# Two cross-attention layers in float32: the last batch's mean from an extra product column, and a bias sum moved from VectorE to ScalarE and adding transfers

## The chip, the cores and the metric

The kernel runs on one core of a Trainium2 chip. The metric is device time in microseconds: the time of one execution of the whole program, input loads and output stores included. Its median over three runs is compared. Beside these times there is one profiled execution, with a record of every instruction of every engine; its span, from first to last record, is shorter than its device time.

A core has TensorE (PE, with PEld for the loading of its stationary operand), VectorE (DVE), ScalarE (ACT) and GpSimd (POOL). SyncE (SP) here only issues transfers; ScalarE and GpSimd issue some too. Each engine takes its own instructions in order and waits at semaphores for the others.

## The reference

There are 8 batches of 100 queries with 1024 features, and a context of 1444 rows of 512 features for each batch. Everything is float32.

```
layer 0:  Q = x Wq + bq;  K = c Wk + bk;  V = c Wv + bv
          x = x + (softmax over keys of (Q K^T / 32)) V Wo + bo
layer 1:  q = x Wq + bq;  k = c Wk + bk;  v = c Wv + bv
          w = softmax over QUERIES of (q k^T / 32)
          x = w v + x
          out = (x - mean) * (var + 1e-6)^-1/2 * gamma + beta    (over the 1024 features)
```

Mean and variance of a query need all 1024 features of its row. The kernel uses that Q K^T = x (Wq Wk^T) c^T plus bias terms and that the value path is (softmax c)(Wv Wo) plus bias terms, so it first multiplies the weights with each other. The term bv Wo, a vector of 1024, belongs to the output bias of layer 0. It is the sum over 1024 rows of Wo, each times one element of bv.

## The kernel before

**Stages.** In order of time: Wq Wk^T of layer 0 (`weight_products`, "qk0", to 52 us), Wv Wo of layer 0 ("vo0", 52 to 100 us), the projected queries of layer 0 ("g0", 100 to 137 us), Wq Wk^T of layer 1 ("qk1", to 184 us), the scores, softmax and weighted rows of layer 0 for the 8 batches (to about 350 us), the last of the value projection of layer 0 (`project0`, "o0", to 381 us), the projected queries of layer 1, and then the batches of layer 1. There the batches form the sets 0 to 3, 4 to 6 and 7. For each batch `alternated` interleaves, on TensorE, the weighted rows of this batch (A) with the scores of the batch two ahead (s). After the first two sets `project1` multiplies their A with Wv; for the last batch `project_last` does it.

**The order of the work.** TensorE's order is the order in which the Python code issues products (`manual_schedule`). For the other engines the framework orders instructions by its own estimate, except for those that are kept in program order: VectorE's between `vector.in_order = True` and `False` (all go through the helper on line 96), and some of ScalarE's. A tile comes from a pool with a number of buffers; the first writer of a reused buffer waits for the last reader of what was in it. The pool `stream` has 10 buffers, for weights, context rows and context columns; in layer 1 two of them hold gamma, beta and the value bias.

**Products with fewer multiplications.** The large products are split in 2x2 blocks and made with seven block products instead of eight. That needs sums of blocks (S1.., T1..) on VectorE before a product, and evictions that put or add one PSUM result into several output blocks. For vo0 (lines 464 to 530) the products come in the order X, Z, Y, X again, and then W and Q, which are split once more and interleaved with a last product into X. The second X product reads S2, four tiles that overwrite S1, which the Y product before it reads, and T2. `put` copies a result by ScalarE, `add` adds it by VectorE. In `project0` (lines 1082 to 1090) one of the seven products, W, is split again in seven steps. The steps x, z, y, x, w, y, x share three PSUM banks; `run(W)` issues the steps that are left.

**The bias sum.** `transferred_sum` makes bv Wo as eight scaled tiles of 128x1024. For "qk1" ScalarE scales all eight (`scaled_sum`) and transfers that add into SBUF, issued by GpSimd (`transfer_added`, line 567), sum them as a tree. For "qk0" and "vo0" ScalarE and such transfers do four; VectorE does the other four in `second_half`, one multiplication and three multiply-adds into one tile, which a last transfer adds to the first. In vo0 `second_half` is called between T2 and the addition of Z. The transposing sum that uses the result (`block_sums`, "bvo") runs in the g0 stage.

**The last batches.** `untransposed` turns x back to queries by features with eight transposes on TensorE and adds the value bias (line 1192, z, two halves of 512). `normalise` follows: statistics by VectorE (line 1198), aggregated (1203), the variance plus epsilon (1205), the power -1/2 on GpSimd (1206), then (z - mean) gamma on VectorE (1207). For all batches but the last, ScalarE multiplies by the power (1209), GpSimd adds beta (1210) and the output leaves (1212). Batches 4, 5 and 6 are finished while A of batch 7 is made. For batch 7 `project_last` makes A Wv in three parts of 512, 384 and 128 columns (1232), adds each to z (1233) and takes its statistics; after the power VectorE makes the two output halves (1215), whose transfers SP and ScalarE issue (1216).

Of the kernel before, what the change touches and what calls it, by code (L numbers as in the profile page):

```python
# [25 lines left out]
F32 = mybir.dt.float32  # L26
AF = mybir.ActivationFunctionType
ALU = mybir.AluOpType
# [27 lines left out]
def two_layer_cross_attention(ctx: ExitStack, tc: tile.TileContext, a: dict, out: bass.AP):  # L56
# [17 lines left out]
    def unit(name):  # L74
        return stream.tile([P, E + L], F32, tag="unit", name=name)
# [4 lines left out]
    def row(name):  # L80
        return work.tile([P, E], F32, tag="row", name=name, bufs=3)
# [58 lines left out]
    def run(*parts):  # L140

        parts = list(parts)
        while parts:
            parts = [g for g in parts if next(g, parts) is not parts]
# [202 lines left out]
    def weight_products(name, left, right, l_width, r_width, scaled, between=None):  # L347
# [87 lines left out]
        def put(r, c, banks):  # L435
            for j in range(2):
                nc.scalar.copy(block(r, c, j), banks[j].rearrange("p (n w) -> p n w", n=per))  # L437

        def add(r, c, banks):
            for j in range(2):  # L440
                to = block(r, c, j)
                vector.tensor_tensor(to, to, banks[j].rearrange("p (n w) -> p n w", n=per), ALU.add)
# [21 lines left out]
        if name == "vo0":  # L464
            accumulate(1)
        put(0, 0, X)
        vector.in_order = name == "vo0"
        combine(T1, B12, B11, ALU.subtract)
        if name == "qk0":
# [26 lines left out]
        if name != "qk0":  # L496
            T2, T4 = B11, B21
            combine(T2, B22, T1, ALU.subtract)
            if name == "vo0":
                accs[scaled[0][0]][1]()  # L500
            add(0, 0, Z)
        combine(S1, S1, A11, ALU.subtract)
        S2 = S1
        if name != "vo0":
            combine(A21, A11, A21, ALU.subtract)
        if name != "qk0":
# [36 lines left out]
    def transferred_sum(name, srcs, of):  # L543

        n = EC if of == "qk1" else EC // 2
        tiles = [row(f"{name}_{n}") for n in range(2)] + [weight_rows(f"{name}_2")[:, :E]]
        tiles += [t[:, :E] for t in prob]  # L550
        if n == EC:
            tiles += [weight_rows(f"{name}_{n}")[:, :E] for n in range(6, 8)]
        scaled_sum(tiles[:n], srcs[:n])

        def second_half():
            t = tiles[n]
            for i, (src, by) in enumerate(srcs[n:]):
                if i == 0:
                    vector.tensor_scalar(t, src, by, None, ALU.mult)
                else:  # L560
                    vector.scalar_tensor_tensor(t, src, by, t, ALU.mult, ALU.add)
            transfer_added(tiles[0], t)

        return tiles[0], second_half
# [4 lines left out]
    def scaled_sum(tiles, srcs):  # L569

        for t, (src, by) in zip(tiles, srcs):
            tc.keep_in_program_order(nc.scalar.activation(t, src, AF.Copy, scale=by))
        k = 1
        while k < len(tiles):
            for i in range(0, len(tiles) - k, 2 * k):
                transfer_added(tiles[i], tiles[i + k])
            k *= 2
# [435 lines left out]
    def project0(AS, A0):  # L1013
# [65 lines left out]
        add(1, 1, 1, Y)  # L1079
        product(X_, S_[1], T2, False)  # L1080

        next(W)
        add(1, 0, 1, X_)
        run(W)
        add(1, 0, 1, Y)
# [62 lines left out]
    def project1_sums(w):  # L1148
        t = weights.tile([P, LC, E], F32, tag="w", name="wv1_s")
        A = [[w[:, 2 * k + i, h * 512 : h * 512 + 512] for i in range(2)] for h in range(2) for k in range(2)]  # L1150
        S = [[t[:, n, i * 512 : i * 512 + 512] for i in range(2)] for n in range(4)]
        left_sums(A, S, engine=nc.gpsimd)
        return A, S
# [38 lines left out]
            nc.vector.scalar_tensor_tensor(z[:, half], bv1[j][:T], s["r"], ps[:T, :], ALU.mult, ALU.add)  # L1192
        yield

    def statistics(s, j, part, parts):
        if j == 0:
            s["stats"] = small.tile([T, parts, 6], F32, tag=f"stats{parts}", name=f"stats_{s['b']}")
        nc.vector.bn_stats(s["stats"][:, j, :], s["z"][:, part])

    def normalise(s):  # L1200
        b, z = s["b"], s["z"]
        mv = small.tile([T, 2], F32, tag="mv", name=f"mv_{b}")
        nc.vector.bn_aggr(mv, s["stats"].rearrange("p a n -> p (a n)"))
        rstd = small.tile([T, 1], F32, tag="rstd", name=f"rstd_{b}")
        nc.vector.tensor_scalar(rstd, mv[:, 1:2], EPS, None, ALU.add)  # L1205
        nc.gpsimd.tensor_tensor(rstd, rstd, mhalf[:T], ALU.pow)  # L1206
        nc.vector.scalar_tensor_tensor(z, z, mv[:, 0:1], gamma[:T], ALU.subtract, ALU.mult)
        if b < B - 1:
            nc.scalar.activation(z, z, AF.Copy, scale=rstd)  # L1209
            nc.gpsimd.tensor_tensor(z, z, beta[:T], ALU.add)  # L1210

            (nc.gpsimd if b < SETS[1][0] else nc.sync).dma_start(out=out[b], in_=z)
            return
        for half, queue in ((slice(0, E // 2), nc.sync), (slice(E // 2, E), nc.scalar)):
            nc.vector.scalar_tensor_tensor(z[:, half], z[:, half], rstd, beta[:T, half], ALU.mult, ALU.add)
            queue.dma_start(out=out[b][:, half], in_=z[:, half])

    def finish(s):

        yield from untransposed(s)  # L1220
        for j in range(2):
            statistics(s, j, slice(j * 512, (j + 1) * 512), 2)
        normalise(s)

    def project_last(s, A):

        parts = (slice(0, 512), slice(512, 896), slice(896, E))
        for j, part in enumerate(parts):
            n = part.stop - part.start
            ps = bank(f"ol_{j}")  # L1230
            for k in range(LC):
                nc.tensor.matmul(ps[:T, :n], A[:, k, :T], wv1[:, k, part], start=(k == 0), stop=(k == LC - 1))
            nc.vector.tensor_tensor(s["z"][:, part], s["z"][:, part], ps[:T, :n], ALU.add)
            statistics(s, j, part, len(parts))
        normalise(s)


    batches = [{"b": b} for b in range(B)]
# [94 lines left out]
    for bs in SETS:  # L1333
        t = wide(f"A1T_{bs[0]}").rearrange("p c t -> p (c t)")[:, : LC * len(bs) * T]
        t = t.rearrange("p (c t) -> p c t", c=LC)
        for i, b in enumerate(bs):
            for n, _ in enumerate(alternated(b, 1, softmax1, t[:, :, i * T : (i + 1) * T])):
                if b % 2 and n == (8 if b == B - 1 else 27):
                    weight_totals(batches[b - 1 : b + 1])
                if (b, n) in finished:  # L1340
                    finishing.append(finish(batches[finished[b, n]]))
                finishing = [f for f in finishing if next(f, finishing) is not finishing]
            if b == 1:
                AS = project1_sums(wv1)
        if b < B - 1:

            between, room = {3: (batches[5], (0, 3, 3, 3, 3)), 6: (batches[7], (1, 0, 0, 1, 2))}[b]
            project1(bs, *AS, t, between["softmax"], room)
    run(untransposed(batches[B - 1]))
    project_last(batches[B - 1], t)  # L1350


# [22 lines left out]
```

## Time and profile before

| | us |
|---|---|
| median of three runs (633.78 to 634.80) | 634.42 |
| the profiled execution | 634.84 |
| its span | 632.9 |
| TensorE busy | 621.5 (98%) |
| VectorE busy | 487.1 (77%) |
| ScalarE busy | 163.9 (26%) |
| GpSimd busy | 102.2 (16%) |

The granted clock of TensorE is 0.997 of full speed. Transfers move 138.27 MB, a mean of 218 GB/s.

How to read it: a line of a timeline has the start and the duration in us, engine, line of the code, operation, output <- inputs, shapes and the count of merged instructions. In square brackets stands how long the engine stood idle before, and for whom. A float32 product is two matmul records for each pair of tiles, so "x16" are eight products. Line 96 is the helper of all VectorE instructions that can be kept in order, so these are told apart by their tiles. Durations of neighbours on one engine overlap by some 0.1 us. A line of the waits has engine, waiting tile and line <- engine, tile and line waited for, then us in total, times, and the longest.

### The profile page before, as it was taken

What the parts mean: (1) busy time and instruction counts of PE and PEld (TensorE: products, weight loads), DVE (VectorE), ACT (ScalarE), POOL (GpSimd) and SP (SyncE); (2) the same over time, 40 slices, a digit from 0 to 9 for tenths busy, and PEclk for the clock granted to TensorE, in tenths of its full rate; (3) what the DMA queues carried; (4) which work ended last, traced back from release to release, by engine and by line L of the source; (5) the groups of instructions that cost most, each with busy time, mean ns of one, the idle gap of its engine ahead of it and who ended that gap; (6) DMA issues with size and microseconds to landing.
All of it is one profiled execution on the core that took longest, in us unless ns stands there. A gap on an engine that the chain in (4) does not pass through costs nothing.

```text
span 632.9 us, 10570 instructions
## 1 busy us (share of the span) xinstructions
PE 621.5 (98%) x4142; PEld 534.2 (84%) x4142; DVE 487.1 (77%) x995; ACT 163.9 (26%) x380; POOL 102.2 (16%) x133
## 2 busy tenths in 40 slices
PE   9999999999999999999999999999999999999994
PEld 8886467688985999999989666756999999999992
DVE  2987979996885797666758687968777659898886
ACT  1322012324304234423230001113433240325301
POOL 2110101112230000000000001008111220544054
PEclk9999999999999999999999999999999999999998
DMA  8969848335999788988942308255888990599002
GB/s 272 293 136 348 274 140 272 68 81 111 203 315 382 283 311 299 327 307 306 312 155 88 101 0 325 96 194 192 295 305 307 316 324 2 201 330 332 27 22 84
DMA packets 52521, 138.27 MB, mean 218 GB/s; under 512 B 4403, under 2 KB 8755, under 8 KB 52471
## 3 DMA queue, kind: packets, MB, share of 16 engines
q1 hardware_dynamic: 46792, 120.85, 55.1%
q0 software_dynamic: 5280, 16.26, 11.7%
q8 instruction: 33, 0.54, 0.3%
q10 hardware_dynamic: 398, 0.47, 0.2%
q14 instruction: 18, 0.14, 0.1%
HBM read 123.36 MB, written 3.28 MB: 200 GB/s over the span
## 4 chain that ended last, share of the span: by engine, by line
PE 90%; DMA 3%; DVE 3%; issue 1%; POOL 1%; ACT 0%; POOLq 0%; DVEq 0%; SPq 0%
PE s L923 25%; PE A L894 25%; PE qk_x L163 6%; PE o_x L163 5%; PE g_x L163 4%; DMA vo<-in_L_xattn_Wo 3%; PE o_y L163 3%; PE g_y L163 3%; PE vo_x L163 2%; PE qk_y L163 2%; PE qk_z L163 2%; DVE vo L96 1%; PE o_z L163 1%; PE o_w L163 1%; PE qk_w L163 1%
## 5 line engine op out<-in xcount | busy, mean ns | idle before, releaser
L894 PE MATMUL A<-w,c 120*128 120x100 f32 (+1 forms) x1536 | 249.6, 265 | 0.0
L894 PEld LDWEIGHTS A<-w,c 120*128 120x128 f32 (+1 forms) x1536 | 218.0, 190 | 2.8
L96 DVE STREAM_TRANSPOSE w<-prob 32x384 f32<-32x384 f32 (+1 forms) x256 | 143.7, 561 | 27.6 <-ACT prob L962 9.7
L923 PE MATMUL s<-cT,g1T 128*100 128x131 f32 (+2 forms) x592 | 122.8, 296 | 0.0
L923 PE MATMUL s<-cT,g0T 128*100 128x131 f32 (+2 forms) x592 | 122.7, 296 | 0.0
L923 PEld LDWEIGHTS s<-cT,g1T 128*100 128x100 f32 x592 | 78.4, 167 | 8.6 <-issue 0.3
L923 PEld LDWEIGHTS s<-cT,g0T 128*100 128x100 f32 x592 | 78.2, 167 | 8.4 <-PE c L593 0.4
L935 ACT ACTIVATE prob<-s,c 100x393 f32<-100x393 f32 (+2 forms) x64 | 34.5, 560 | 112.7 <-PE s L923 99.5
L1111 ACT ACTIVATE w<-w,negmax 120x100 f32<-120x100 f32 (+1 forms) x96 | 34.8, 364 | 82.7 <-DVE negmax L96 82.7
L955 DVE TENSOR_REDUCE maxima<-prob 100x1 f32<-100x394 f32 (+3 forms) x32 | 16.5, 528 | 23.4 <-ACT prob L935 23.1
L1321 POOL DMA_DIRECT2D wv<-in_L_xattn_Wv x1 | 0.8, 772 | 191.2 <-PE o_x L163 191.2
L163 PE MATMUL qk_x<-qk 128*128 128x256 f32 x128 | 29.7, 380 | 0.0
L1130 POOL TENSOR_TENSOR part<-w 120x500 f32<-120x500 f32 x8 | 10.9, 1368 | 112.9 <-DVE rstd L1205 28.6
L163 PEld LDWEIGHTS qk_x<-qk 128*128 128x128 f32 x128 | 23.3, 190 | 3.0 <-ACT qk L437 0.2
L669 ACT ACTIVATE g1T<-g_x,k 128x400 f32<-128x400 f32 x4 | 2.4, 594 | 69.2 <-PE g_x L163 69.0
L1111 ACT ACTIVATION_READ_ACCUMULATOR w<-w,negmax 120x1 f32 (+1 forms) x96 | 17.9, 187 | 0.0
L1210 POOL TENSOR_TENSOR z<-z,vectors 100x1024 f32<-100x1024 f32 x7 | 16.5, 2356 | 8.2 <-ACT z L1209 8.2
L96 DVE TENSOR_TENSOR xT<-xT,o_x 128x400 f32<-128x400 f32 (+1 forms) x32 | 15.8, 539 | 2.2 <-PE o_x L163 2.0
L1188 PE MATMUL z<-ident,xT 128*100 128x128 f32 x64 | 16.3, 273 | 0.0
L1209 ACT ACTIVATE z<-z,rstd 100x1024 f32<-100x1024 f32 x7 | 8.0, 1149 | 31.9 <-POOL rstd L1206 31.9
L1192 DVE SCALAR_TENSOR_TENSOR z<-vectors,r,z 100x512 f32<-100x512 f32 x16 | 11.8, 740 | 4.8 <-PE z L1188 4.8
L163 PE MATMUL vo_x<-vo 128*128 128x512 f32 x32 | 15.3, 595 | 0.0
(415 smaller groups left out, 987.8 us busy)
## 6 DMA issues: line engine op xcount, KB each, us to landing
cT<-in_ctxT SPq DMA_DIRECT2D x64, 722.0 KB, 6.3
c<-in_ctx SPq DMA_DIRECT2D x48, 768.0 KB, 8.3
c<-in_ctx SPq DMA_DIRECT2D x16, 512.0 KB, 5.9
vo<-in_L_xattn_Wo SPq DMA_DIRECT2D x8, 512.0 KB, 10.1
qk<-in_L_xattn_WqT SPq DMA_DIRECT2D x8, 512.0 KB
qk<-in_L_xattn_WqT SPq DMA_DIRECT2D x15, 256.0 KB, 5.8
c<-in_ctx SPq DMA_DIRECT2D x16, 224.0 KB, 5.9
xT<-in_xT SPq DMA_DIRECT2D x2, 1600.0 KB
```

The lines of the kernel that those rows point to most:

```text
L96: ins = getattr(nc.vector, op)(*args, **kw)
L163: nc.tensor.matmul(banks[n // per][:, n % per * width : (n % per + 1) * width], lhs[i][:, n * P : (n + 1) * P], rhs[i], start=(fresh and i ...
L894: nc.tensor.matmul(ps[:, k * T : (k + 1) * T], c[m // CQ][:r, m % CQ, k * P : (k + 1) * P], w[:r, m, :], start=(m == 0 and k == 0), stop=( ...
L923: nc.tensor.matmul(banks[n // per][:T, cuts[n] - o : cuts[n + 1] - o], q[:, k, t0 : t0 + T], cT[k][:, cuts[n] : cuts[n + 1]], start=(k == ...
L935: nc.scalar.activation(p[:, part], ps[:T, : part.stop - part.start], AF.Identity, bias=key_bias[layer][:T, b : b + 1], scale=SCALE,)
L955: nc.vector.tensor_reduce(maxima[:, n : n + 1], p[:, part], AX.X, ALU.max)
L1111: nc.scalar.activation(w[:r, m0 + m, :], w[:r, m0 + m, :], AF.Exp, bias=negmax[:r, m : m + 1], accum_out=total[:r, m : m + 1])
L1130: add(part, w[:MR, 0:5, :], w[:MR, 5:10, :], ALU.add)
L1188: nc.tensor.transpose(ps[:T, e * P : (e + 1) * P], xT[:, 4 * j + e, b * T : (b + 1) * T], ident)
L1192: nc.vector.scalar_tensor_tensor(z[:, half], bv1[j][:T], s["r"], ps[:T, :], ALU.mult, ALU.add)
L1209: nc.scalar.activation(z, z, AF.Copy, scale=rstd)
L1210: nc.gpsimd.tensor_tensor(z, z, beta[:T], ALU.add)
```

## The change

1. vo0: the second four tiles of the bias sum are scaled by ScalarE, right after it has put the first product, and summed by three more adding transfers; VectorE's four instructions are gone. The addition of Z moves behind the four instructions that make S2. Two of the tiles take buffers of `weight_rows`.
2. project0: four steps of W rather than one are issued ahead of the addition of X_, so VectorE's two additions of X_ come after W's first four.
3. Layer 1: after the work of batch 6, `last_columns` copies the first 383 columns of Wv into a new tile and puts the row sums of Wv, by ScalarE's accumulator, in the 384th column. In the built order these five instructions stand among the evictions of batch 7's scores. The two tiles come from `stream`.
4. `project_last`: parts of 383 (with the extra column, 384), 512 and 129 columns. The mean comes from the extra column and two ScalarE sums of z. Each part is centred as it comes, squared and summed by ScalarE; the parts are multiplied by gamma meanwhile. The statistics instructions, the aggregate and the full-width (z - mean) gamma are gone. A last ScalarE instruction forms the variance, GpSimd takes the power.
5. `normalise` for batch 6: the multiplication by the power and the addition of beta are one VectorE instruction, instead of ScalarE's and GpSimd's. In the built order it stands on VectorE between the two instructions that make the mean of batch 7.

```diff
@@ weight_products @@
         put(0, 0, X)
+        if name == "vo0":
+            accs[scaled[0][0]][1]()
         vector.in_order = name == "vo0"
...
             combine(T2, B22, T1, ALU.subtract)
-            if name == "vo0":
-                accs[scaled[0][0]][1]()
-            add(0, 0, Z)
+            if name != "vo0":
+                add(0, 0, Z)
         combine(S1, S1, A11, ALU.subtract)
         S2 = S1
+        if name == "vo0":
+            add(0, 0, Z)
@@ transferred_sum @@
-        if n == EC:
+        if of != "qk0":
             tiles += [weight_rows(f"{name}_{n}")[:, :E] for n in range(6, 8)]
         scaled_sum(tiles[:n], srcs[:n])
         def second_half():
             t = tiles[n]
-            for i, (src, by) in enumerate(srcs[n:]):
...
+            if of != "qk0":
+                scaled_sum(tiles[n:], srcs[n:])
+            else:
+                for i, (src, by) in enumerate(srcs[n:]):
...
             transfer_added(tiles[0], t)
@@ project0 @@
-        next(W)
+        run(islice(W, 4))
         add(1, 0, 1, X_)
         run(W)
@@ normalise @@
         nc.vector.scalar_tensor_tensor(z, z, mv[:, 0:1], gamma[:T], ALU.subtract, ALU.mult)
-        if b < B - 1:
+        if b == B - 2:
+            nc.vector.scalar_tensor_tensor(z, z, rstd, beta[:T], ALU.mult, ALU.add)
+        else:
             nc.scalar.activation(z, z, AF.Copy, scale=rstd)
             nc.gpsimd.tensor_tensor(z, z, beta[:T], ALU.add)
...
@@ new @@
+    def last_columns(w):
+        unused, got = unit("wv_unused"), unit("wv_first").rearrange("p (k n) -> p k n", k=LC)
+        n = got.shape[2] - 1
+        nc.scalar.copy(got[:, :, :n], w[:, :, :n])
+        for k in range(LC):
+            nc.scalar.activation(unused[:, :E], w[:, k, :], AF.Copy, accum_out=got[:, k, n:])
+        return got
@@ project_last @@
-        parts = (slice(0, 512), slice(512, 896), slice(896, E))
...
+        z, centred = s["z"], row("centred")[:T]
+        n0 = first.shape[2] - 1
+        parts = (slice(0, n0), slice(n0, n0 + 512), slice(n0 + 512, E))
...
+        for j in range(2):
+            nc.scalar.activation(unused, z[:, j * 512 : (j + 1) * 512], AF.Copy, accum_out=zs[:, j : j + 1])
+        vector.in_order = True
+        def scaled(part):
+            vector.tensor_tensor(z[:, part], centred[:, part], gamma[:T, part], ALU.mult)
         for j, part in enumerate(parts):
...
-            nc.vector.tensor_tensor(s["z"][:, part], s["z"][:, part], ps[:T, :n], ALU.add)
-            statistics(s, j, part, len(parts))
-        normalise(s)
+            if j == 0:
+                vector.scalar_tensor_tensor(mean, ps[:T, n : n + 1], zs[:, 0:1], zs[:, 1:2], ALU.add, ALU.add)
+                vector.tensor_scalar(mean, mean, 1.0 / E, None, ALU.mult)
+            vector.scalar_tensor_tensor(centred[:, part], ps[:T, :n], mean, z[:, part], ALU.subtract, ALU.add)
+            nc.scalar.activation(unused[:, :n], centred[:, part], AF.Square, accum_out=sq[:, j : j + 1])
+            if j == 0:
+                scaled(part)
+        vector.tensor_tensor(v, sq[:, 0:1], sq[:, 1:2], ALU.add)
+        vector.tensor_scalar(v, v, 1.0 / E, EPS, ALU.mult, ALU.add)
+        for part in parts[1:]:
+            scaled(part)
+        nc.scalar.activation(v, sq[:, 2:3], AF.Identity, bias=v, scale=1.0 / E)
+        nc.gpsimd.tensor_tensor(rstd, v, mhalf[:T], ALU.pow)
+        for half, queue in ((slice(0, E // 2), nc.sync), (slice(E // 2, E), nc.scalar)):
+            vector.scalar_tensor_tensor(z[:, half], z[:, half], rstd, beta[:T, half], ALU.mult, ALU.add)
+            queue.dma_start(out=out[B - 1][:, half], in_=z[:, half])
@@ main loop, layer 1 @@
+        if b == B - 2:
+            first = last_columns(wv1)
```

## The prediction

> **What bounds the kernel now.** First the page's chain that ended last, by engine:
>
> ```profile
> PE 90%; DMA 3%; DVE 3%; issue 1%; POOL 1%; ACT 0%; POOLq 0%; DVEq 0%; SPq 0%
> ```
>
> Nine tenths of the span is TensorE itself, so an edit off TensorE counts where TensorE stands still and after its last product. The waits of PE name every such place:
>
> ```profile
> PE warm L108 <- DVE ones L105: 1.1, 1, 1.1
> PE vo_x L163 <- DVE vo_s L96: 1.0, 1, 1.0
> PE o_w_y L163 <- DVE xT L96: 0.6, 1, 0.6
> PE g_z_x L163 <- DVE g_t L96: 0.4, 1, 0.4
> ```
>
> The change touches the second and third. From 184 us to 616 us no wait for a transfer is listed: what TensorE gains early is not given back to a load there. The second place, in PE's timeline and VectorE's:
>
> ```profile
> 74.20 7.10 PE L163 MATMUL vo_x<-vo,vo_s 128*128 128x512 f32 x16 [1.04 <-DVE vo_s L96]
> ```
>
> ```profile
> 67.82 0.74 DVE L96 TENSOR_SCALAR prob<-vo,L_xattn_bv 128x1024 f32<-128x1024 f32 x1
> 68.60 3.92 DVE L96 SCALAR_TENSOR_TENSOR prob<-vo,L_xattn_bv,prob 128x1024 f32<-128x1024 f32 x3
> 72.44 1.28 DVE L96 TENSOR_TENSOR vo<-vo,vo_z 128x512 f32<-128x512 f32 x2
> 73.63 1.43 DVE L96 TENSOR_TENSOR vo_s<-vo_s,vo 128x256 f32<-128x256 f32 x4
> ```
>
> The four sums vo_s that the next product reads stand behind four bias instructions and two additions of Z. The third place, PE's timeline and then VectorE's:
>
> ```profile
> 374.31 0.50 PE L163 MATMUL o_w_w<-o_t,vo 128*128 128x200 f32 x2
> 375.37 0.60 PE L163 MATMUL o_w_y<-o_t,o_t 128*128 128x200 f32 x2 [0.56 <-DVE xT L96]
> ```
>
> ```profile
> 373.73 1.05 DVE L96 TENSOR_TENSOR xT<-xT,o_x 128x400 f32<-128x400 f32 x2
> 374.69 0.35 DVE L96 TENSOR_TENSOR xT<-xT,o_w_z 128x200 f32<-128x200 f32 x1
> 374.96 0.35 DVE L96 TENSOR_TENSOR xT<-xT,o_w_y 128x200 f32<-128x200 f32 x1
> ```
>
> The second o_w_y product adds into a bank that is read at 374.96 to 375.31, after two wide additions of o_x. Last the end, from the timeline of all engines:
>
> ```profile
> 618.43 2.35 POOL L1210 TENSOR_TENSOR z<-z,vectors 100x1024 f32<-100x1024 f32 x1 [1.86 <-ACT z L1209]
> 618.72 3.14 DVE L1207 SCALAR_TENSOR_TENSOR z<-z,mv,vectors 100x1024 f32<-100x1024 f32 x1
> ...
> 626.10 0.15 DVE L1205 TENSOR_SCALAR rstd<-mv 100x1 f32<-100x1 f32 x1 [0.46 <-DVE mv L1203]
> 626.17 1.28 DVE L1207 SCALAR_TENSOR_TENSOR z<-z,mv,vectors 100x1024 f32<-100x1024 f32 x1
> 626.33 1.52 POOL L1206 TENSOR_TENSOR rstd<-rstd,mhalf 100x1 f32<-100x1 f32 x1 [0.46 <-DVE rstd L1205]
> 627.89 1.41 DVE L1215 SCALAR_TENSOR_TENSOR z<-z,rstd,vectors 100x512 f32<-100x512 f32 x2 [0.44 <-POOL rstd L1206]
> ```
>
> TensorE ends at 624.54; the output instruction starts at 627.89, and from there to the end nothing is changed.
>
> **What the Trainium skill says.** "SBUF — State Buffer", Who interferes with whom: a VectorE instruction with two SBUF inputs and a GpSimd instruction that reads SBUF exclude each other for a whole instruction. The trace agrees: L1207 takes 1.28 us alone and 3.14 us behind the addition that GpSimd ends at 620.78; the power on L1206, 0.57 us in its quickest rows, takes 1.52 us and ends 0.40 us after L1207 does. "DMA: Bandwidth & Descriptors", SWDGE vs HWDGE vs iDMA: adding transfers are issued by GpSimd alone, so new ones queue on POOL; all those here are there, at 0.85 us of issue each. "ScalarE: Activation LUTs", What ACT_TABLE_LOAD costs: a change of function set costs 1283 ns for the load. The trace has one such load, 1283 ns, at the start; the changed program still holds one, so Square adds none.
>
> **The bias sum.** Four VectorE instructions go (67.82 to 72.44, 4.6 us). The two Z additions (1.2 us) move behind the four vo_s. Each vo_s overwrites a quarter that the vo_y product reads; that product runs 66.13 to 73.16, so the quarters come free at about 67.9, 69.7, 71.4 and 73.1. VectorE has just finished T2 at 67.8, so the first vo_s is ready at 68.4. The next product can follow at 73.16, and needs the fourth quarter only at 73.16 + 3 x 1.76 = 78.4. Gain: the whole 1.04. Late next: Z, at 73.6 to 74.9, then T4 to 77.3 as before; the first product on T4 moves from 81.14 to 80.10, still covered. VectorE idles 2.16 us before 81.77 and 0.96 before 84.00, so its work from there starts 1.04 earlier with TensorE, through the chain at 98.9 to 107.
>
> In exchange ScalarE gets four 128x1024 multiplications (1.15 each), from 60.06 to about 64.9: the last waits for the row that VectorE shows landed at 63.46. Queued behind them on ScalarE is the eviction of vo_y, which waits for TensorE until 72.34: 7.4 us of cover. T4 now also waits for these reads, done 10 us before. POOL issues three more transfers (four instead of one, 0.85 each) behind the one at 63.37. They run in a chain of three, at 7.2 to 8.4 us each (the page's DMA issues for such tiles): 64 + 3 x 8.4 = 89 at worst. The next POOL issue waits until 108.0 and the sum is transposed later still. They share the engines with xT and weights; these are busy until about 77 and idle from 80 to 85 (windows of the DMA share). Each adds 0.5 MB read and written, at 326 GB/s some 5 us in all, and xT is first multiplied at 100.2. Cost: nothing, on 11 us of cover.
>
> **The order in the projection.** W's four steps now precede the two o_x additions, all the same instructions. VectorE then reads the o_w_y bank as soon as it is full, 374.13 to 374.48, not 374.96 to 375.31. The product can start at 374.31 + 0.34 = 374.65 against 375.37: 0.72. The o_x additions end their first bank at about 375.31; the o_x product wants it at 375.33, so 0.02 to 0.1 is given back. Gain: 0.7. VectorE's other additions end near 378.0, before the wait for o_q_x, which moves to about 378.7.
>
> **The extra column.** last_columns puts a copy of 4x383 on ScalarE (nearest row: 100x1444 in 1.50 us, so 1.57) and four 1024-wide sums (1.15, and 0.19 for the accumulator row). In the built order the copy and three sums stand among the four evictions of the last scores. Their buffer comes free with the third part of those scores, at about 572.3; ScalarE reaches the copy at 574.23. The work is 1.57 + 3 x 1.34 = 5.6 us, of which 1.9 fills idle time, and overlap of neighbours takes up to 1 us more: the last eviction ends at 581.1 to 582.1, not 578.38. VectorE's 16 transposes (0.59) wait for it; batch 3's normalisation now goes first, into that wait. They end at 590.7 to 591.5, not 589.6. The sums for the projection and the maxima are late by that, but VectorE idles 0.29, 1.06 and 0.37 us between 595 and 599 and makes it up; the exponentials end by 599.1, before their third use at 600.8. The weights are ready at 601.6 as before, and TensorE uses them at 603.76. Two stream buffers less: the last batch's rows are issued at about 577 to 584 rather than 572 to 580; at 8.3 us to landing they are in by 592. Cost: nothing, with 2 us of cover.
>
> **The tail.** TensorE's work is one column longer. On VectorE, L1207 of batch 6 still ends at 621.86. Then the mean's first step, and batch 6's last multiplication, which used to be ScalarE's and GpSimd's: it waits for the power (622.27) and takes 1.28, to 623.59. Only then: mean scaled 623.66; first part centred (0.58) 624.28; times gamma (0.56) 624.88; second part (0.74) 625.54; third (0.28) 625.74. ScalarE squares the second part, 0.61 and 0.19, by 626.35. VectorE adds and scales, 626.74; then gamma on two parts, 627.53. ScalarE's last 100x1 step ends at 627.1, but the power is shut out until 627.53 and ends 0.40 later, 627.93; output starts at 627.97 against 627.89. Cost +0.1. No row shows a square, a 100x1 ScalarE step or these hand-offs. From below, with batch 6's instruction elsewhere, the chain runs from TensorE's end: 624.6 + 0.28 + 0.1 + 0.5 + 0.4 + 0.3 + 0.6, about 626.8, that is -1.1. From above: seven of the hand-offs have no row; at the 0.46 idle seen before L1205 instead of some 0.05, they add 7 x 0.41 = 2.9, that is +3.0. I take +0.1, since other dependent pairs start 0.03 to 0.1 apart.
>
> **Sum.** -1.04 - 0.7 + 0.1 = -1.64. The profiled execution took 634.84 with a span of 632.9, so 633.2 and 631.3; the median of the three runs is 634.42, 0.42 lower, so 632.8.
>
> **Rivals.** First, one gap does not close: the four multiplications or another reader hold T4 or a bank, and the wait reappears under another name. Without the 1.04 the time is 633.8, without the 0.7 it is 633.5. For it: VectorE is nearly full from 84 to 98. Against: 10 us of cover. Second, the tail is dear: the hand-offs above cost their upper price, +3.0, which gives 634.42 - 1.74 + 3.0 = 635.7. From 1.74 on the tail takes back everything. For it: the 0.46 was measured in this very tail, and the new chain is longer. Against: that idle time ends just after GpSimd's addition at 625.88, which is gone. In between, +1 to +2 gives 633.7 to 634.7. Third, the tail shortens by 1.1: 631.6; against it stands batch 6's instruction in the built order.
>
> **How the numbers follow.** A difference of 0.2%, 1.27 us, is about what a measurement of this kernel can tell from no change. Forecast 58% (own range 632.2 to 633.1); short tail 6%; one gap open 10%; tail dearer by 1 to 2 us 11%; tail at its upper price or beyond 15%. So faster 0.64, same 0.21, slower 0.15. The range, 631.4 to 634.7, leaves out the dearest tail and a little below.
>
> **What would show it.** Right: PE's waits no longer list vo_x and o_w_y; VectorE shows vo_s straight after T2; the weights of batch 7 are ready before A begins; the interval from TensorE's last product to the output instruction is 3.3 to 3.6 us. Wrong: a new wait of PE near 75, 375 or 604, or a tail over 5 us.

## The result and the profile after

The changed kernel takes 633.82 us (median of 20 runs, 633.06 to 634.53); the kernel before took 635.32 in the same comparison (20 runs). The ratio is 0.9979, 95% interval 0.9973 to 0.9986. A second sample, taken later (below), gave 0.9969, interval 0.9958 to 0.9980. In the first sample the medians differ by 1.50 us, and the ratio amounts to 1.3.

The forecast was 632.8 against 634.42, a ratio of 0.9974, which lies between the two samples; faster was the likeliest outcome. The 632.8 itself is missed by 1.0, because the first three runs of the kernel before, which gave 634.42, lay 0.9 below the median of all its 20. The profiled execution took 633.67, with a span of 631.6.

The waits of PE after:

```profile
PE warm L108 <- DVE ones L105: 1.1, 1, 1.1
PE g_z_x L163 <- DVE g_t L96: 0.4, 1, 0.4
```

Both waits at which the change aimed are gone, and none has come in their place. The vo0 stage, PE's timeline and then VectorE's:

```profile
66.78 7.03 PE L163 MATMUL vo_y<-vo_s 128*128 128x512 f32 x16
73.64 7.03 PE L163 MATMUL vo_x<-vo,vo_s 128*128 128x512 f32 x16
```

```profile
68.69 0.43 DVE L96 TENSOR_TENSOR vo_s<-vo_s,vo 128x256 f32<-128x256 f32 x1 [0.71 <-PE vo_y L163]
...
73.84 0.43 DVE L96 TENSOR_TENSOR vo_s<-vo_s,vo 128x256 f32<-128x256 f32 x1 [1.29 <-PE vo_y L163]
74.19 1.28 DVE L96 TENSOR_TENSOR vo<-vo,vo_z 128x512 f32<-128x512 f32 x2
```

Now each vo_s waits until TensorE has read a quarter, and TensorE no longer waits for vo_s. From vo_y's start to vo_x's it is 73.64 - 66.78 = 6.86 us, which is 16 matmuls at 0.43 with no gap; before it was 74.20 - 66.13 = 8.07. The projection, PE's timeline:

```profile
373.68 0.50 PE L163 MATMUL o_w_w<-o_t,vo 128*128 128x200 f32 x2
374.02 0.56 PE L163 MATMUL o_w_y<-o_t,o_t 128*128 128x200 f32 x2
```

From o_w_w to o_w_y it is 0.34 us, before it was 1.06. The tail, the timeline of all engines (three dots stand for lines left out):

```profile
617.46 3.15 DVE L1211 SCALAR_TENSOR_TENSOR z<-z,mv,vectors 100x1024 f32<-100x1024 f32 x1
...
621.05 1.28 DVE L1214 SCALAR_TENSOR_TENSOR z<-z,rstd,vectors 100x1024 f32<-100x1024 f32 x1 [0.31 <-POOL rstd L1210]
...
625.16 0.16 DVE L96 TENSOR_TENSOR v<-last 100x1 f32<-100x1 f32 x1 [0.59 <-ACT unused L1264]
...
625.42 0.89 DVE L96 TENSOR_TENSOR z<-centred,vectors 100x512 f32<-100x512 f32 x2
625.60 0.29 ACT L1271 ACTIVATE v<-last,v 100x1 f32<-100x1 f32 x1
625.97 0.55 POOL L1272 TENSOR_TENSOR rstd_last<-v,mhalf 100x1 f32<-100x1 f32 x1 [4.95 <-ACT v L1271]
626.55 1.41 DVE L96 SCALAR_TENSOR_TENSOR z<-z,rstd_last,vectors 100x512 f32<-100x512 f32 x2 [0.25 <-POOL rstd_last L1272]
```

The hand-offs between engines do not carry the dear price of the second rival: the 100x1 steps start 0.2 to 0.4 us after one another. From the start of ol (TensorE's last products) to the output instruction it is 626.55 - 616.23 = 10.32 us, before 627.89 - 617.49 = 10.40.

One thing does not fit the sum. vo_z started at 59.91 in this profile and at 59.27 before, 0.64 later, although no instruction ahead of it has changed; only the later gains make up for it. The experiments had to tell what that is.

### The profile page after: what moved, and what is told of

It is laid out like the page before. It is cut to its first block, busy times and chain, and to the rows that moved or that the text cites. A ratio compares the mean times of both kernels' runs of the same rounds, so it can differ in the third digit from the quotient of the medians.

```text
span 631.6 us, 10604 instructions
## 1 busy us (share of the span) xinstructions
PE 621.8 (98%) x4142; PEld 534.8 (85%) x4142; DVE 482.4 (76%) x993; ACT 175.4 (28%) x403; POOL 101.5 (16%) x135
## 4 chain that ended last, share of the span: by engine, by line
PE 96%; DVE 1%; issue 1%; POOL 1%; ACT 0%; DVEq 0%; POOLq 0%
PE s L929 25%; PE A L900 25%; PE qk_x L163 7%; PE o_x L163 5%; PE g_x L163 4%; PE vo_x L163 3%; PE o_y L163 3%; PE g_y L163 3%; PE qk_y L163 2%; PE qk_z L163 2%; PE o_z L163 1%; PE o_w L163 1%; PE qk_w L163 1%; PE vo_y L163 1%; PE vo_z L163 1%
## 5 line engine op out<-in xcount | busy, mean ns | idle before, releaser
L1217 POOL TENSOR_TENSOR z<-z,vectors 100x1024 f32<-100x1024 f32 x6 | 14.1, 2358 | 8.1 <-ACT z L1216 8.1
L965 ACT ACTIVATE prob<-prob,negmax 100x1444 f32<-100x1444 f32 x8 | 12.0, 1499 | 11.2 <-DVE negmax L963 11.2
```

The costliest lines, as they stand in the source:

```text
L965: nc.scalar.activation(p, p, AF.Exp, bias=negmax, accum_out=total)
```

## The experiments

**The parts alone.** Three kernels carry one part of the change each.

```diff
@@ e1: vo0's bias sum, in the kernel before: weight_products @@
         put(0, 0, X)
+        if name == "vo0":
+            accs[scaled[0][0]][1]()
...
-            if name == "vo0":
-                accs[scaled[0][0]][1]()
-            add(0, 0, Z)
+            if name != "vo0":
+                add(0, 0, Z)
...
         S2 = S1
+        if name == "vo0":
+            add(0, 0, Z)
@@ e1: transferred_sum @@
-        if n == EC:
+        if of != "qk0":
...
+            if of != "qk0":
+                scaled_sum(tiles[n:], srcs[n:])
@@ e2: the order in the projection, in the kernel before @@
-        next(W)
+        run(islice(W, 4))
@@ e3: the last batch's column and tail as in the whole change, in the kernel before @@
+        if b == B - 2:
+            first = last_columns(wv1)
...
-        if b < B - 1:
+        if b == B - 2:
+            nc.vector.scalar_tensor_tensor(z, z, rstd, beta[:T], ALU.mult, ALU.add)
```

> Kernel before with the bias sum alone changed: vo0's four multiplications by ScalarE, three more adding transfers, and Z added behind the four sums vo_s. The outputs are computed in full. Theory: the wait of vo_x is gone, and the product vo_x starts 6.87 us after vo_y (16 matmuls at 0.43) instead of 8.07, so the time falls by 1.2 us (the prediction's term said 1.04); the o_w_y wait of 0.56 stays. Rival 1 (the gap does not close): PE lists a wait of about 1 us at vo_x or at the first products on T4 near 80, and the time is within 0.2 us of before.

> Kernel before with one edit: four steps of W are taken ahead of the two o_x additions in the projection, instead of one. The outputs are computed in full. Theory: o_w_w to o_w_y falls from 1.06 to about 0.34 us, and the time by 0.7 us. Rival 1: the o_x bank comes free later and the o_x product takes the wait over, and the time is within 0.2 us of before.

> Kernel before with the last batch's mean from one more column, its parts centred and squared as they come, and batch 6's last step on VectorE; vo0's sum and the order in the projection are as before. The outputs are computed in full. Theory: 0.1 us more (the prediction's term) to 0.1 us less (the interval from TensorE's last product to the output instruction in the trace of the whole change), with no new wait of PE at the last batch. Rival 2 (dear tail): 1.7 to 3.0 us more. Rival 3 (tail shortens): 1.1 us less.

Measured against the kernel before, as ratios: the bias sum 0.9998 (0.9990 to 1.0006), the order 0.9992 (0.9984 to 1.0000), the last columns 0.9997 (0.9989 to 1.0004). At the places themselves the first two did what was expected: vo_y to vo_x is 74.19 - 67.33 = 6.86 in the first, o_w_w to o_w_y 0.34 in the second. The last columns cost nothing that can be measured. But the bias sum, with its gap closed (6.86 us instead of 8.07), left the time where it was, and this contradicts both its theory and rival 1, since no new wait of PE is listed. In its profile qk_z, the second product of the kernel, started at 12.50; in the first profile of before at 11.31.

**The start.** Is the late start the program's own, and does it eat the gain?

```diff
@@ e8: the kernel before, no edit.  e9: as e1.  e11: the whole change, no edit. @@
@@ e10: e1 with the edit of e2 @@
-        next(W)
+        run(islice(W, 4))
```

> The kernel before, unchanged, run as if it were an experiment: a ratio within 0.1% of 1. Its second profile tells whether the start of a program is its own or chance. In the first profile the product qk_z, the second one of the kernel, starts at 11.31, in the bias sum alone at 12.50 (it waits for the first weights to land; no instruction ahead of it is changed), and that 1.19 us is what the bias sum's gain of 1.2 us is missing at TensorE's end. Theory (the start belongs to the program): 11.3 again within 0.2. Rival (it is drawn anew in each execution): anywhere from 11.3 to 12.5.

> The bias sum alone, a second time. The outputs are computed in full. Theory (the start belongs to the program): qk_z at 12.5 within 0.3 again, vo_y to vo_x again 6.87, and a time within 0.3 us of before, as in the first sample. Rival (drawn anew): qk_z elsewhere between 11.3 and 12.5, and a time that falls by up to 1.2 us against before.

> Kernel before with the bias sum and the order in the projection, without the last batch's column and tail. The outputs are computed in full. By the spacings of TensorE alone it is 1.2 + 0.7 = 1.9 us faster. If the start belongs to the program and changes with any edit, the time is 1.9 less whatever the start gives or takes: qk_z's start beside it says how much, and the time less that start falls by 1.9 us within 0.3. Rival (the parts don't add up for a reason on TensorE): a wait is listed that neither part alone shows.

> The whole change, a second time. The outputs are computed in full. Its first profile has qk_z at 11.95. Theory (the start belongs to the program): 11.95 within 0.2 again, and a ratio of 0.998. Rival (drawn anew): elsewhere between 11.3 and 12.5, with the same ratio as a mean over executions. Against the kernel with bias sum and order alone, less the start of each, it should differ by the tail alone: 0.1 us either way.

The theory of these four expectations fell. qk_z started at 12.73 in the kernel before and at 11.21 in the bias sum, just the other way round than in the first pair; in the whole change at 11.35 instead of 11.95. The start is drawn anew in each execution, between 11.2 and 12.7 in the fourteen profiles. The product before it, qk_x, took 7.07 us in the first profile of before and 8.27 in the second, while the first weights were still being loaded. That their landing sets the start is argued, not shown: no wait of PE for a transfer is listed there.

A time less its start (device time of the profiled execution minus the start of qk_z) is therefore the better measure. In the two profiles of the whole change all of the start reaches the end: 633.67 - 11.95 = 621.72 and 633.06 - 11.35 = 621.71. In the kernel before it does not: 634.84 - 11.31 = 623.53 and 635.25 - 12.73 = 622.52. The second profile of the kernel before shows why. Its waits of PE, all of them:

```profile
PE warm L108 <- DVE ones L105: 1.1, 1, 1.1
PE o_w_y L163 <- DVE xT L96: 0.6, 1, 0.6
PE g_z_x L163 <- DVE g_t L96: 0.4, 1, 0.4
```

In the unchanged kernel the wait of vo_x is absent. VectorE's timeline, then PE's, of the same profile:

```profile
63.79 0.69 DVE L96 TENSOR_TENSOR vo<-vo,vo 128x512 f32<-128x512 f32 x1 [1.02 <-DMA vo<-in_L_xattn_Wo]
...
73.97 1.42 DVE L96 TENSOR_TENSOR vo_s<-vo_s,vo 128x256 f32<-128x256 f32 x4
```

```profile
67.56 7.03 PE L163 MATMUL vo_y<-vo_s 128*128 128x512 f32 x16
74.53 5.82 PE L163 MATMUL vo_x<-vo,vo_s 128*128 128x512 f32 x13
```

VectorE waits here for a row of Wo to land, and from then on works without a pause to vo_s. From that first instruction to vo_x it is 74.53 - 63.79 = 10.74 us; in the first profile of before 74.20 - 63.46 = 10.74, and in the profile of the projection's order (e2) 74.39 - 63.65 = 10.74. TensorE for its part could begin vo_x 61.69 us after qk_z (73.64 - 11.95 in the changed kernel, where nothing holds it).

So the wait is the difference between two times: 10.74 us after VectorE's instruction, which follows a landing, and 61.69 us after the start. The two are not independent, but the instruction began anything from 51.1 to 52.2 us after qk_z in the fourteen profiles, and the wait varies with this distance. Taken as the excess of vo_y to vo_x over 6.87 it is 1.20, 0.10, 1.04 and 1.11 in the four profiles of kernels with the old bias sum (before twice, the order, the last columns), a mean of 0.86. In the ten profiles with the new order of vo0 the same working says what the old order would have waited: 0.3 to 1.2. Over all fourteen the mean is 0.7; this is an estimate, since it takes the 10.74 to hold there too.

The bias sum's second sample gave 0.9995 (0.9986 to 1.0003), bias sum and order together 0.9985 (0.9979 to 0.9992). The kernel before against itself gave 0.9994 (0.9986 to 1.0002), which tells how little a difference of 0.05% means. No wait of PE is listed that a part alone doesn't show, so the rival for the two parts together fell too.

**What the bias sum alone loses at the end.** A mean gain of 0.86 us, 0.14%, is still more than the 0.02% and 0.05% of its two samples. From the start of ol to the end of the span before takes 632.9 - 617.49 = 15.4 us (15.5 in its second profile), the bias sum alone 633.4 - 617.45 = 15.95 (again 15.95 in its second, and 15.98 with the order added), the whole change 15.4 in both profiles. The tail of the bias sum alone, all engines' timeline:

```profile
625.71 0.15 DVE L1211 TENSOR_SCALAR rstd<-mv 100x1 f32<-100x1 f32 x1
...
627.49 1.41 DVE L1221 SCALAR_TENSOR_TENSOR z<-z,rstd,vectors 100x512 f32<-100x512 f32 x2 [0.44 <-POOL rstd L1212]
```

The idle time of 0.46 that the kernel before has ahead of L1205, the same instruction, at 626.10 is not there, so the output starts 627.49 - 617.45 = 10.04 us after ol and not 10.40. Yet the span ends 5.91 after the start of the output instruction, not 5.01. Batch 6's output leaves at 626.14 here (the end of SP's row for three outputs, 614.40 + 11.74), and the last batch's first half at 628.27, 2.13 us later; in before 2.48 lie between. The DMA share tells the two parts of this: the last bytes move until 631.8 here, 4.3 us after the output instruction's start, and until 631.7 in before, 3.8 after it, so 0.5 to 0.6 is transfers; the other 0.3 lies behind the last byte (1.5 us to the end of the span, before 1.2). In e4 (vo0's order alone, below), where the output also starts 10.04 after ol, only the first part shows: 5.6 us to the end.

Why the 0.46 is missing in every program with vo0's order changed, and present in the others with the old tail, the runs don't tell: the instruction, what it waits for and its tiles are the same. GpSimd's addition, which the prediction named, is not it: in the bias sum alone it runs from 623.49 to 625.84, and L1211 starts at 625.71. With these 0.55 us more at the end, the bias sum is worth -0.86 + 0.55 = -0.3 us, and with the order -0.3 - 0.64 = -0.95: the samples gave 0.02% and 0.05% of 635 us, 0.1 and 0.3, and 0.15%, 0.95. The agreement is no proof, since the intervals of these ratios are some 0.5 us wide to either side. By the time less the start the two samples of the bias sum give 622.69 and 622.74, the kernel before without its wait 623.53 - 1.20 = 622.33 and 622.52 - 0.10 = 622.42, so the loss at the end is rather 0.3 to 0.4: part of the 0.55 is not in the device time (outside the span lie 1.8 us, in before 1.9). Bias sum and order give 622.11, 0.40 above the whole change where 0.1 was expected.

**Batch 6 on ScalarE and GpSimd again.** This asked what edit 5 costs in the chain, and it met the same collision.

```diff
@@ e5: normalise, in the changed kernel @@
-        if b == B - 2:
-            nc.vector.scalar_tensor_tensor(z, z, rstd, beta[:T], ALU.mult, ALU.add)
-        else:
-            nc.scalar.activation(z, z, AF.Copy, scale=rstd)
-            nc.gpsimd.tensor_tensor(z, z, beta[:T], ALU.add)
+        nc.scalar.activation(z, z, AF.Copy, scale=rstd)
+        nc.gpsimd.tensor_tensor(z, z, beta[:T], ALU.add)
@@ e12: e5, and @@
+        if b != B - 2:
             (nc.gpsimd if b < SETS[1][0] else nc.sync).dma_start(out=out[b], in_=z)
```

> The changed kernel with batch 6's last step given back to ScalarE (multiplication by rstd) and GpSimd (addition of beta); all else as changed. The outputs are computed in full. Theory: the instruction of 1.28 us on VectorE stands in the chain between TensorE's last product and the output, so without it the first centring starts about 1.2 us earlier and the tail is shorter by up to 1.1 us (the prediction's lower bound of the tail); GpSimd's addition shares SBUF with VectorE's gamma instructions and gives some of it back: 0.3 to 1.1 us faster than the changed kernel, 0.65 likeliest. Rival: the chain is held by TensorE's last column and the statistics behind it, and the time does not move, or GpSimd's addition shuts the gamma instructions or the power out and it is up to 1 us slower.

> The changed kernel with batch 6's last step given back to ScalarE and GpSimd, and batch 6's output not sent at all: its 400 KB are left out, so the output lacks that batch. With the transfer, from the last output instruction of VectorE to the end of the span took 5.94 us, against 5.05 in the changed kernel, where batch 6's output is issued 1.9 us earlier. Theory (the last batch's two transfers share the engines with batch 6's): without it these 5.94 us become 5.0, the time from TensorE's first tail product ol to the output instruction stays 9.65, and the kernel is about 0.9 us faster than with it. Rival (the longer end has another cause, such as the earlier issue of the two transfers): 5.9 again, and the same time.

The ratio of the first is 0.9979 (0.9971 to 0.9987), that of the whole change; its time less its start is 633.25 - 11.52 = 621.73, against 621.72. The chain did get shorter as expected: ol to output 625.46 - 615.81 = 9.65 us instead of 10.32. It went into the end of the program. The timelines of the two kernels, with batch 6's output in the first line, the last batch's in the others; first e5, then the changed kernel:

```profile
612.76 11.76 SPq L1215 DMA_DIRECT2D out<-z  x3
...
626.24 0.29 SPq L1271 DMA_DIRECT2D out<-z  x1
```

```profile
613.18 9.47 SPq L1219 DMA_DIRECT2D out<-z  x3
...
627.33 0.29 SPq L1275 DMA_DIRECT2D out<-z  x1
```

The first row ends with the issue of batch 6's 400 KB: at 624.52 in e5, 1.72 us ahead of the last batch's; at 622.65 in the changed kernel, 4.68 ahead. From the output instruction to the end it is 5.94 and 5.05, so e5 loses 0.89 for the 0.67 it gained. The span less the start is therefore some 0.2 longer than in the changed kernel. The device time less the start is not, since it has 1.8 us outside the span there and 2.1 in the changed kernel. The windows of the DMA share (from, to, length, busy of PE, PEld, DVE, ACT, POOL, granted clock, DMA share, GB/s) of e5:

```profile
626.00:628.00 2.00, 0.00 (x0) 0.00 (x0) 0.88 (x2) 0.00 (x0) 0.00 (x0) 0.50 0.57 192
```

and of the changed kernel:

```profile
626.00:628.00 2.00, 0.00 (x0) 0.00 (x0) 1.72 (x4) 0.00 (x0) 0.52 (x1) 0.67 0.00 0
```

With batch 6's transfer left out, the end took 5.44 us, and the time less the start fell to 632.51 - 11.28 = 621.23. The ratio is 0.9972 (0.9963 to 0.9981), too near to that of e5 to tell the two apart. So sharing the engines with batch 6's output is 0.50 of the 0.89 us, and 0.39 stayed. The theory was half right.

The traces show where the 0.39 lies: the last bytes move until 629.05, 3.8 us after the output instruction, just as in the changed kernel (630.34) and not 4.4 as in e5 (629.85); from there to the end of the span it is 1.62 us here, 1.57 in e5 and 1.25 in the changed kernel. It is time behind the last transfer, when the engines only close the program; why that takes longer in some of the programs is open.

For the change this means that edit 5 costs 0.67 in VectorE's chain and gives about as much back by sending batch 6 two microseconds earlier: with it and without it the time is the same.

**The order without the move.** Was it VectorE's place in the queue, or the work itself?

```diff
@@ e4: weight_products, in the kernel before @@
-            if name == "vo0":
-                accs[scaled[0][0]][1]()
-            add(0, 0, Z)
+            if name != "vo0":
+                add(0, 0, Z)
...
         S2 = S1
+        if name == "vo0":
+            accs[scaled[0][0]][1]()
+            add(0, 0, Z)
```

> Kernel before with nothing but the order of VectorE's work changed at vo0: the bias sum (its four instructions) and the additions of Z stand behind the four sums vo_s; the bias sum stays with VectorE. The outputs are computed in full. If the place in VectorE's queue is what made TensorE wait, the wait of vo_x is gone as in the whole change (vo_x 6.87 us after vo_y). What the move to ScalarE is worth then shows at T4: VectorE has its bias sum from about 73.6 to 78.2, Z to 79.4 and T4 to 81.8, where TensorE wants T4's first part at about 80.1. Theory: a new wait of 0.5 to 1.7 us at the first products on T4, so a total between 0.7 us faster and 0.5 us slower than before. Rival: order is all that counts and the time falls by 1.2 us as with the work moved.

Slower: 1.0029 (1.0018 to 1.0039). vo_y to vo_x is 6.87 here too, so the order alone closes the gap. The work comes due later, as the waits of PE show:

```profile
PE vo_q_x L163 <- DVE vo L96: 1.1, 1, 1.1
...
PE vo_w_x L163 <- DVE vo L96: 0.2, 1, 0.2
```

The two come to 1.3 us; the products around them lose a little each, too little for the view to list. The first products on T4 wait 0.2 us, which falls short of the expected 0.5 to 1.7; the larger part of the bill comes at 97.5 us. By its timeline VectorE works from 73.53 to 100 us without a listed pause, where in before it stood idle for 2.16 and 0.96. TensorE is 0.86 behind the first profile of before at vo_q_x and 1.18 three products later, after having been 0.87 ahead at vo_x: 2.05 lost for 1.2 gained. Against a kernel before with its mean wait of 0.86 that makes 1.2 us; the ratio says 1.8, with 0.6 to either side. The 4.6 us had to leave VectorE, and could not just be put off.

**The cover of the last columns.**

```diff
@@ e7: the evictions of the scores of batch 7, in the changed kernel @@
+        again = 10 if (layer, b) == (1, B - 1) else 1
...
+            for _ in range(again if n == len(parts) - 1 else 1):
                 nc.scalar.activation(p[:, part], ps[:T, : part.stop - part.start], AF.Identity, ...)
```

> The changed kernel with the last eviction of the last batch's scores issued ten times instead of once, nine more of 0.47 us each on ScalarE: 4.3 us more in the place where the column's copy and sums stand; the outputs are computed in full. It measures the cover. The prediction gave 2 us of cover to the weights of batch 7, ready at 601.6 and used at 603.76 by the product A. If that is where the cover ends, PE lists a wait of about 2.3 us at A of batch 7 and the time rises by that. The trace of the changed kernel points to an earlier place: the transposes would end near 593.2, and the sums o_t ready at 589.15, which PE reads for o_y at 592.30, would be ready at about 593.5, so PE would wait some 1.2 us there, and 1.2 us in all. If neither holds, no wait and no change.

Slower: 1.0078 (1.0062 to 1.0094). The place is the one that the trace pointed to; the size is not. Waits of PE, and VectorE's timeline:

```profile
PE o_y L163 <- DVE o_t L96: 3.8, 1, 3.8
```

```profile
586.62 9.45 DVE L96 STREAM_TRANSPOSE w<-prob 32x384 f32<-32x384 f32 x16 [7.11 <-ACT prob L943]
596.11 0.54 DVE L96 TENSOR_TENSOR o_t<-A1T 128x150 f32<-128x150 f32 x2
```

In the changed kernel the transposes start at 579.39. Less the start of each program they came (586.62 - 12.42) - (579.39 - 11.95) = 6.76 us later, not 4.3, since ScalarE's copy of A, its fourth sum and batch 3's multiplication now went in ahead of the repeated evictions. The time less the start rose by (639.86 - 12.42) - 621.72 = 5.72 us: 3.8 is the listed wait, and the products of o_y behind it then took 3.95 us instead of 2.21. So the cover is 6.76 - 5.72 = 1.0 us. It ends where VectorE's sums o_t, which stand behind the transposes, are read by o_y; the product A of batch 7 has no wait.

**A better version.** The changed kernel has another lock in the tail: batch 6's centring (L1211) takes 3.15 us at 617.46 beside GpSimd's addition of 2.35 for batch 5.

```diff
@@ e6: normalise, in the changed kernel @@
-        if b == B - 2:
+        if b in (B - 3, B - 2):
```

> The changed kernel with batch 5's last step on VectorE as batch 6's is, so GpSimd has no addition of a whole row left beside VectorE's instruction of batch 6 (3.15 us at 617.46, of which GpSimd's addition of 2.35 us holds it up). The outputs are computed in full. Theory: VectorE saves some 1.9 us of lock and pays 1.28 us for the added instruction, so the chain behind it starts about 0.6 us earlier and the time falls by 0.6 us. Rival: the chain waits for TensorE's last column and not for VectorE, or the added instruction delays batch 6: no change, or up to 1.3 us slower.

The ratio to before is 0.9974 (0.9964 to 0.9984), the median 632.90. In the timeline of VectorE in this kernel:

```profile
618.38 1.27 DVE L1211 SCALAR_TENSOR_TENSOR z<-z,mv,vectors 100x1024 f32<-100x1024 f32 x1
620.10 1.28 DVE L1214 SCALAR_TENSOR_TENSOR z<-z,rstd,vectors 100x1024 f32<-100x1024 f32 x1 [0.31 <-POOL rstd L1210]
625.60 1.42 DVE L96 SCALAR_TENSOR_TENSOR z<-z,rstd_last,vectors 100x512 f32<-100x512 f32 x2 [0.25 <-POOL rstd_last L1272]
```

The centring takes its 1.27, ol to output is 9.64 instead of 10.32, and the end stays at 5.0 because both outputs still leave early. Its time less its start, 632.68 - 11.65 = 621.03, is 0.69 below the whole change: the expected 0.6. It is the fastest complete kernel of this study by that measure; by the intervals of the ratios alone it can't be told from the whole change.

## Why the prediction was right, and where it was not

The direction and the size were right. Of the sum's three terms two were well founded; that their sum also arrived at the end was in part luck, since the prediction had left the last transfers out.

- **The order in the projection, -0.7.** Right to its parts: the gap fell by 0.72, and from o_w_w to g_x, the first product after the stage, it is 380.04 - 373.68 = 6.36 us against 381.31 - 374.31 = 7.00, so 0.64, with 0.08 given back.
- **The bias sum, -1.04.** Right in mechanism, mis-sized in two ways. In its own profile the gap was 1.20, not 1.04: the idle time in the bracket counts from the modelled end of the matmuls (66.13 + 7.03 = 73.16), while 16 of them follow each other in 6.87. And the wait is not a constant of the kernel: it was 0.10 to 1.20 in four profiles, with a mean of 0.86 (0.7 by the estimate over fourteen). The step "Gain: the whole 1.04" took one profiled execution's wait for that of every execution, although the trace of before showed that VectorE's work towards vo_s began with a landing (63.46).
- **What was moved in exchange, nothing.** Right. ScalarE's multiplications ran 60.6 to 64.9. GpSimd's last adding transfer was issued at 84.53, after a wait of 11.97 us at the one before. One of the transfers took 13.0 us to land, more than the 8.4 assumed, but within the cover: the next one is issued at 107.38. T4 was in time: no wait of PE there.
- **The last columns, nothing.** The cost was right, but the cover was 1.0 us by measurement where "2 us of cover" was said, and the place was another. The step looked at A of batch 7, which uses the weights, and passed over the sums o_t in the same VectorE queue, whose lateness it called made up by idle time.
- **The tail, +0.1.** It was -0.08 to the output instruction, and nothing (15.4 us before and after) to the end. The chain was worked out well: the gamma instructions were to end 627.53 - 617.49 = 10.04 us after ol, and ended 626.31 - 616.23 = 10.08 after it. The step that failed is "the power is shut out until 627.53": the power took 0.55 us from 625.97 while VectorE's two gamma instructions ran from 625.42 to 626.31. The Trainium skill's rule in "SBUF — State Buffer", Who interferes with whom, which carried that step, shows in full on L1211 (3.15 us beside an addition, 1.27 alone) and did not hold this power until both instructions were over: it began when the first of them had 0.13 us left, and ended 0.21 after the second, not 0.40. Size alone does not exempt an instruction: in e5 the 100x1 sum v took 0.60 us instead of 0.16 and ended with GpSimd's addition, at 624.2. What the prediction left out is the transfers: it said that from the output instruction "to the end nothing is changed", but that stretch is 5.0 to 5.9 us in these programs, by when batch 6's output leaves and by how long the closing takes. In the whole change it is 5.0, so the two gains arrive; with the bias sum and the order under the old tail it is 5.9, and part of them is lost. Edit 5 keeps the stretch short, but costs as much in the chain.
- **Rivals.** No gap came back under another name, so the first fell, though the bias sum by itself ended where that rival would have put it, by way of the tail. The dear tail fell: no hand-off showed the 0.46, though not for the reason given, GpSimd's addition that is gone. The third rival's condition, "with batch 6's instruction elsewhere", was tried: it gives 0.67 to the output instruction, where 1.1 was the most, and nothing at the end.

The terms with these sizes give -0.86 - 0.64 + 0 = -1.5 us, or -1.3 with the 0.7. By the medians the first sample gave -1.5 and the second 633.63 - 635.31 = -1.68. As times, both parts together are clear of no change (0.9985) and the order alone is at the edge (0.9992); the bias sum's part by itself shows only in the traces.

## What to carry to other kernels

Before a wait is put into a sum, follow it back to its origin. Here that was a transfer's landing, and the waiting engine had a start of its own, so the wait came out anew in each execution; a second profile of the same kernel showed it. Where the start of the program varies like this, compare kernels by the time less a common early landmark, and set shifts in a trace against the same landmark. And count the last output's transfer together with the output before it: here a chain made shorter by 0.67 us gave nothing, chiefly because the earlier output was then still in flight.

## What was not expected of the hardware

- The second product of one and the same program started at 11.31 and at 12.73 us, with no edit; in all fourteen profiles the range is 11.2 to 12.7.
- The end of 5.94 us in e5 has 0.50 us for sharing the engines with 400 KB issued 1.72 us ahead of the last two transfers of 200 KB. Another 0.39 us lies behind the last byte, for a cause that stays open.
- A GpSimd power of 100x1 took 0.55 us when it began 0.13 us before the end of the first of two VectorE instructions with two SBUF inputs each, and 1.52 us beside one of 1.28 us in the kernel before.
- Adding transfers of 512 KB within SBUF took up to 13.0 us from issue to landing when three of them were on the way, against at most 7.8 us for the last two of vo0 in the kernel before, which went one at a time.
